# Span-attention steps moved to other stretches by their TensorE tiling, and the fourth group's projections in four column tiles

## The chip, the cores and the metric

The kernel runs on one core of one Trainium2 chip. The metric is the device time of one execution in microseconds (us), as the median of several runs. The engines that matter are TensorE (PE; its weight loads are shown apart as PEld), VectorE (DVE), ScalarE (ACT) and GpSimd (POOL). SyncE (SP) only issues DMAs.

## The reference

The input is `x` (32 batches of 64 rows, 256 wide) and a context of 32 batches of 1601 keys. Three blocks follow each other, each added to `x`, each after a layer norm; all of it in float32.

```python
# 1. cross attention, 16 heads of 16: the 64 rows of a batch look at its 1601 keys
qh, kh, vh = heads(ln(x) @ wq.T + bq), heads(ctx @ wk.T + bk), heads(ctx @ wv.T + bv)
x = x + softmax(mask(qh @ kh.T / 4)) @ vh @ wo.T + bo
# 2. span attention among the 64 rows of a batch
span, value = ln(x) @ W_span.T, heads(ln(x) @ W_val.T)
mean, soft = sigmoid(span[..., 0]) * 64, softplus(span[..., 1])
x = x + softmax(-soft * (pos - mean) ** 2) @ value @ W_out.T
# 3. feed forward: one shared gated unit and two of eight experts per row, chosen by the row's number
x = x + ((silu(h @ sw1 + sb1) * (h @ sw3 + sb3)) @ sw2 + sb2 + experts(h)) / 2
```

Most of the work is in block 1: the projections of 32 x 1601 keys and values, the scores, their exponentials and the product with the values.

## The kernel before, in words

**Halves and groups.** The main loop (L678) runs over 63 of 64 "halves": batch `b` of 32, and in it the heads' half `c` (0 or 1). A half has eight heads in four pairs. The keys are cut into 13 blocks of 124, and the blocks into four groups of 4, 3, 3 and 3 (`GROUPS`). In turn `n` of the loop the scores of half `n + 1` are made while half `n` is turned into probabilities and half `n - 1` is multiplied by its values. Each turn has four parts, g = 0 to 3; the text calls them **stretches** and numbers them `4 * n + g`.

**TensorE's work in a stretch, in the order of the program.** (1) `scores` (L470), tile `psc`: for each key block four matmuls with 32 rows of the array each, one pair of heads in each row tile, into four PSUM banks. (2) In g = 0: four transposes of the running maximum (`pm`, L515), the projection of the next batch's keys of group 0 (`pk`, L443), and four transposes that spread the maximum along rows (`pb`, L530); then `values(n - 1, 1)` (L554, tile `pvs`), the second half of the product with the values. (3) In g = 1 to 3: `project_keys` of group g (`pk`), and in some stretches `project_values` (`pv`, L459); in g = 3 two of these. (4) `run(4 * n + g)`: steps of other work that are due. After g = 3 comes `values(n, 0)` at the head of the next turn.

**Three tilings of TensorE.** The scores use the array as four row tiles (32 x 128). The product with the values, and the product `po2` of the span attention, use it as four column tiles (128 x 32); `pval` (L244) uses two column tiles (128 x 64). Everything else, all projections and transposes included, uses the whole array. A float32 matmul of the program is two matmul instructions in the profile, each with its weight load, so `pk` in one stretch is four instructions, and a column or row tiled product of four tiles is eight.

**VectorE's work.** For each group, the four additions of the mask (L487), which also take the scores out of PSUM, with up to three running maxima (L508) in between; the last three maxima of a half follow g = 3, and the last of them writes `mx`, which the transposes `pm` read. In g = 0 it takes the column maxima (L522). ScalarE takes `pk` and `pv` out of PSUM and computes the exponentials; GpSimd subtracts the maxima (L539, 3.7 us for one pair of heads).

**The agenda.** Work on 128-row tiles of `x` (two batches) is written as generators: `span_steps` (L209; block 2 and the norm of block 3), `query_steps` (L401; the norm and the query projection of block 1) and `finish_steps` (L621; dividing by the sums, and the transposes to `oT`). A step runs in the stretch that the agenda names, and what it yields says after how many stretches the next one runs. So the order of every engine's instructions is fixed by hand (`manual_schedule`). Since a tile has two batches of two halves, everything repeats every four turns. With turns counted as `n mod 4`, the steps of one tile fall as follows (stretch counted from the turn with `n mod 4 = 0`; 16 and above are in the next round, where the next tile's first steps run as well):

| step, tiles | before |
|---|---|
| `po` (L213), VectorE's addition and norm statistics | 2 |
| norm (ACT), then transposes `tr_h`, then `psp` and `pval` with copies to `vbd` | 3, 4, 5 |
| `z` exponential; twenty small VectorE operations (L271 to L287) | 6; 8 |
| subtract, square and weigh, least, exponential, total (POOL, ACT, DVE) | 9 to 13 |
| transposes `psa` (L315); `po2` (L325) | 15; 16 |
| `po3` (L335) with VectorE's addition and statistics | 17 |
| norm (ACT); transposes `tr_f` (L201) with two VectorE copies (L346) | 18; 19 |
| query: statistics, norm, `tr_q`, `pq` (L413), bias | 5, 6, 7, 8, 9 |

**PSUM.** Six banks are shared by all tiles that `mm_bank` (L92) gives out. Two more hold the sums with the values and the running maximum. A tile's first matmul waits until the bank's last reader is done: VectorE's addition for `psc`, ScalarE's copy for `pk` and `pv`.

**The end.** After the last turn a written-out sequence (L728 to L760) runs the remaining steps between units of the shared feed-forward; then the experts follow (L807 to L841).

## Time and profile before

| | |
|---|---|
| median of 3 runs | 1612.97 us (1610.87 to 1616.4) |
| the profiled execution: its own time, its span | 1611.86 us, 1609.8 us |
| mean granted TensorE clock | 0.993 |
| PE, PEld busy | 96%, 72% of the span |
| DVE, POOL, ACT busy | 78%, 69%, 56% |
| turns of the main loop with n mod 4 = 0, 1, 2, 3 (for n = 16 to 19) | 23.37, 21.94, 22.60, 21.92 us |

The last row is the distance between the starts of the first scores of successive turns, read from TensorE's timeline (391.79, 415.15, 437.09, 459.69 and 481.61 us). An engine's busy share is a mean over the whole span; a wait between two engines shows in the list of waits and in the timeline.

### The profile page before, as it was taken

How to read it: one execution, taken by the hardware profiler on the slowest of the kernel's cores; microseconds unless marked ns; L12 is line 12 of the kernel's file. 1: busy time of each engine (PE TensorE's matmuls, PEld its weight loads, DVE VectorE, ACT ScalarE, POOL GpSimd, SP SyncE). 2: the span in 40 equal slices, each digit the busy share in tenths (PEclk: the TensorE clock that was granted, in tenths of full speed). 3: DMA queues.
4: the chain of work that ended last, by engine and by line, in shares of the span. 5: the costliest groups of instructions: out<-in, count | busy, mean ns of one | idle time of the engine just before them, and what ended most of it. 6: DMA issues, size and time to landing. Idle time of an engine off the chain costs nothing.

```text
span 1609.8 us, 55500 instructions
## 1 busy us (share of the span) xinstructions
PE 1548.2 (96%) x24996; PEld 1159.3 (72%) x24996; DVE 1260.5 (78%) x2700; ACT 900.4 (56%) x1229; POOL 1118.8 (69%) x424
## 2 busy tenths in 40 slices
PE   8999999999999999999999999999999999998999
PEld 5777777777777777777777777777777777764588
DVE  4888879888887889888888879888887889886300
ACT  3555656565665656565565656565565656556411
POOL 1777768768696768768687768868687768862620
PEclk9999999999999999999999999999999999999999
DMA  5111111111110111111111111111111111104200
GB/s 170 55 31 43 34 40 34 49 44 43 49 43 28 43 40 33 50 43 43 50 43 37 36 39 34 49 44 43 49 43 32 39 37 34 34 3 130 78 24 30
DMA packets 52044, 73.32 MB, mean 46 GB/s; under 512 B 3812, under 2 KB 51040, under 8 KB 51680
## 3 DMA queue, kind: packets, MB, share of 16 engines
q1 hardware_dynamic: 50992, 69.00, 14.6%
q8 instruction: 196, 3.21, 0.8%
q10 hardware_dynamic: 816, 0.79, 0.1%
q14 instruction: 40, 0.33, 0.1%
HBM read 65.57 MB, written 4.19 MB: 43 GB/s over the span
## 4 chain that ended last, share of the span: by engine, by line
PE 59%; DVE 37%; issue 2%; ACT 1%; DMA 1%; POOL 0%; ACTq 0%; SPq 0%; DVEq 0%; POOLq 0%
DVE mrun L508 13%; DVE prob L487 13%; PE pv L459 13%; PE pk L443 13%; PE pvs L554 9%; PE psc L478 8%; PE py L832 3%; PE u L583 3%; PE pm L515 2%; PE ph L814 2%; PE pb L530 1%; DVE total L305 1%; DVE least L300 1%; DVE mrun L285 1%; PE pval L244 1%
## 5 line engine op out<-in xcount | busy, mean ns | idle before, releaser
L539 POOL TENSOR_TENSOR prob<-prob,mb 124x1664 f32<-124x1664 f32 x252 | 934.1, 3725 | 323.9 <-ACT mb L534 317.1
L487 DVE TENSOR_TENSOR prob<-psc,madd 124x384 f32<-124x384 f32 (+1 forms) x1024 | 582.2, 582 | 176.0 <-PE psc L478 175.9
L508 DVE TENSOR_TENSOR mrun<-prob,mrun 124x512 f32<-124x512 f32 x704 | 483.4, 687 | 7.0 <-ACT mrun L500 4.0
L443 PE MATMUL pk<-ct,wkT_sb 128*128 128x372 f32 (+2 forms) x1024 | 414.6, 529 | 14.8 <-DMA wkT_sb<-in_wkT 5.3
L544 ACT ACTIVATE prob<-prob 124x1664 f32<-124x1664 f32 x256 | 401.5, 1587 | 15.6 <-POOL prob L539 12.6
L459 PE MATMUL pv<-wvT_sb,ct 128*124 128x256 f32 (+1 forms) x1664 | 388.7, 382 | 0.0
L459 PEld LDWEIGHTS pv<-wvT_sb,ct 128*124 128x124 f32 (+1 forms) x1664 | 313.6, 188 | 80.4 <-DVE prob L487 3.4
L478 PE MATMUL psc<-qbd,kT 32*124 32x128 f32 x6656 | 293.9, 286 | 27.0 <-DVE prob L487 24.1
L478 PEld LDWEIGHTS psc<-qbd,kT 32*124 32x124 f32 x6656 | 230.5, 181 | 102.1 <-DVE prob L487 64.3
L447 ACT ACTIVATE kT<-pk,cols 128x372 f32<-128x372 f32 (+2 forms) x256 | 152.0, 594 | 261.8 <-PE pk L443 261.3
L443 PEld LDWEIGHTS pk<-ct,wkT_sb 128*128 128x128 f32 x1024 | 176.8, 192 | 120.6 <-issue 33.3
L465 ACT COPY v<-pv 124x512 f32<-124x512 f32 (+1 forms) x224 | 124.7, 557 | 222.2 <-PE pv L459 222.2
L554 PE MATMUL pvs<-prob,v 124*17 124x64 f32 x13312 | 212.3, 220 | 0.0
L554 PEld LDWEIGHTS pvs<-prob,v 124*17 124x17 f32 x13312 | 189.9, 98 | 26.9 <-issue 25.4
L834 DVE SCALAR_TENSOR_TENSOR ot<-py,prob 128x256 f32<-128x256 f32 x16 | 6.8, 425 | 75.7 <-PE py L832 75.7
L583 PE MATMUL u<-xfT,sw_sb 128*128 128x512 f32 x128 | 57.4, 599 | 0.4 <-DVE xfT L346 0.4
L530 PEld LDWEIGHTS pb<-cst,mc 128*124 128x124 f32 x256 | 29.6, 134 | 35.7 <-DVE mc L522 30.0
L515 PE MATMUL pm<-cst,mx 124*128 124x124 f32 x256 | 40.3, 280 | 8.7 <-DVE mx L508 7.8
L508 DVE TENSOR_TENSOR mx<-prob,mrun 124x512 f32<-124x512 f32 x64 | 43.9, 686 | 2.2
L821 ACT ACTIVATE hT<-ph,cols 128x256 f32<-128x256 f32 x32 | 13.4, 471 | 56.2 <-PE ph L814 56.2
L583 PEld LDWEIGHTS u<-xfT,sw_sb 128*128 128x128 f32 x128 | 23.6, 190 | 27.4 <-issue 24.8
L522 DVE TENSOR_REDUCE mc<-pm 128x4 f32<-128x496 f32 x64 | 42.5, 664 | 0.8 <-PE pm L515 0.8
(126 smaller groups left out, 1133.7 us busy)
## 6 DMA issues: line engine op xcount, KB each, us to landing
ct<-in_ctxT SPq DMA_DIRECT2D x64, 372.0 KB, 3.2
ct<-in_ctxT SPq DMA_DIRECT2D x32, 496.0 KB, 3.5
ct<-in_ctxT SPq DMA_DIRECT2D x32, 361.0 KB, 3.1
w<-in_w SPq DMA_DIRECT2D x16, 256.0 KB, 6.1
x<-in_x SPq DMA_DIRECT2D x16, 128.0 KB, 2.1
x_kept<-x SPq DMA_DIRECT2D x16, 128.0 KB, 1.7
prob<-x_kept SPq DMA_DIRECT2D x8, 256.0 KB, 5.5
out<-ot SPq DMA_DIRECT2D x16, 128.0 KB, 1.9
```

Of the source, the lines that this page charges most:

```text
L443: nc.tensor.matmul(ps[:, :kn], lhsT=wkT[:, i, c * P : (c + 1) * P], rhs=cts[b][g][:, i, :kn], start=(i == 0), stop=(i == 1),)
L447: nc.scalar.activation(kTs[c][:, k0 : k0 + kn], ps[:, :kn], AF.Identity, bias=cols[:, B_K + c : B_K + c + 1])
L459: nc.tensor.matmul(ps[:kn, n * D : (n + 1) * D], lhsT=cts[b][g][:, i, k0 : k0 + kn], rhs=wvT[:, i, :], start=(i == 0), stop=(i == 1),)
L465: nc.scalar.copy(vs[b % 2][:kn, 2 * u : 2 * u + n, :, :DK], ps[:kn, : n * D].rearrange("p (n h d) -> p n h d", n=n, d=DK),)
L478: nc.tensor.matmul(ps[:CHUNK, k * P : (k + 1) * P], lhsT=kTs[c][32 * j : 32 * j + 32, at : at + CHUNK], rhs=qbd[b // 2][32 * j : 32 * j + ...
L487: nc.vector.tensor_tensor(pair_of(n, j)[:, c0 : c0 + nb, :].rearrange("p k (e q) -> p k e q", e=2), ps[:CHUNK, : nb * P].rearrange("p (k e ...
L508: nc.vector.tensor_tensor(dst, block_of(n, k), run, ALU.max)
L515: nc.tensor.transpose(ps[:, j * CHUNK : (j + 1) * CHUNK], m[:CHUNK, j, :], ident[:CHUNK, :CHUNK])
L539: engine.tensor_tensor(sj, sj, m[:CHUNK, j, None, :].to_broadcast([CHUNK, NKC, P]), ALU.subtract)
L544: nc.scalar.activation(pair_of(n, j), pair_of(n, j), AF.Exp)
L554: nc.tensor.matmul(pvs[32 * j : 32 * j + DK + 1, c, :, r, :], lhsT=v[:kn, k, 8 * c + h, :], rhs=pair_of(n, h // 2)[:kn, k, (h % 2) * S : ( ...
L583: nc.tensor.matmul(ps, lhsT=w[:, c, hc * P : (hc + 1) * P], rhs=xfT[:, c, :, slot], start=(c == 0), stop=(c == 1),)
```

## The change

Four things change. The projections of keys and values in stretches with g = 3 are issued as four column tiles of 32 (the new helper `product`). `pval` is issued as four column tiles of 32 in place of two of 64. The steps of stretch `4 * n` run before `values(n - 1, 1)` and no longer after it. The distances between the steps of `span_steps` come from a table, `WAITS` (for the last two tiles `CLOSE`), the exponential of `z` stands before `pval`, and `query_steps` starts one stretch later.

```diff
+    WAITS = (1, 1, 1, 1, 1, 1, 1, 1, 1, 1, 1, 3, 3, 1, 1, 1)
+    CLOSE = (1, 1, 1, 1, 0, 2, 1, 1, 1, 1, 1, 2, 1, 1, 1, 1)
     def span_steps(t: int, oT):
+        waits = iter(CLOSE if t >= NTILE - 2 else WAITS)
...
-        yield 1
+        yield next(waits)
...
+        yield next(waits)
+        nc.scalar.activation(z, z, AF.Exp, scale=-1.0)
+        yield next(waits)
         pval = mm_bank(f"pval_{t}")
         for b in range(2):
             for c in range(2):
-                for e in range(2):
+                for j in range(4):
+                    e, i = divmod(j, 2)
                     nc.tensor.matmul(
-                        pval[e * S : (e + 1) * S, b * P : (b + 1) * P],
-                        lhsT=hT[:, c, b * S : (b + 1) * S], rhs=wvalT[:, c, e * P : (e + 1) * P],
-                        start=(c == 0), stop=(c == 1), tile_position=(0, e * S),
+                        pval[32 * j : 32 * j + 32, b * P : (b + 1) * P],
+                        lhsT=hT[:, c, b * S + 32 * i : b * S + 32 * i + 32],
+                        rhs=wvalT[:, c, e * P : (e + 1) * P],
+                        start=(c == 0), stop=(c == 1), tile_position=(0, 32 * j),
                     )
...
-        yield 1
-        nc.scalar.activation(z, z, AF.Exp, scale=-1.0)
-        yield 2
+        yield next(waits)
...
+    def product(out, lhsT, rhs, start: bool, stop: bool, tiled: bool):
+        n = lhsT.shape[-1]
+        for at in range(0, n, 32) if tiled else (0,):
+            end = min(at + 32, n) if tiled else n
+            nc.tensor.matmul(
+                out[at:end], lhsT=lhsT[:, at:end], rhs=rhs, start=start, stop=stop,
+                **(dict(tile_position=(0, at)) if tiled else {}),
+            )
...
     def run(stretch: int):
         for steps in agenda.pop(stretch, []):
-            wait = next(steps, None)
+            while (wait := next(steps, None)) == 0:
+                pass
             if wait:
                 agenda[stretch + wait].append(steps)
...
-            agenda[4 * n + 1].append(query_steps(b // 2 + 1))
+            agenda[4 * n + 2].append(query_steps(b // 2 + 1))
...
                 m = maxima_along_rows(turned[1])
+                less_maxima(n, 0, m, nc.gpsimd)
+                run(4 * n)
                 if n:
                     values(n - 1, 1)
...
-                project(project_keys, c, g)
+                project(project_keys, c, g, g == 3)
...
                     for u in range(5 if c else 1, 7 if c else 3):
-                        project(project_values, u)
-            less_maxima(n, g, m, nc.gpsimd)
-            run(4 * n + g)
+                        project(project_values, u, True)
+            if g:
+                less_maxima(n, g, m, nc.gpsimd)
+                run(4 * n + g)
```

In the order in which the two built programs hold TensorE's instructions, the steps then fall so: `tr_h` stays in stretch 4 and `psp` in 5, `pval` goes from 5 to 7, `psa` from 15 to 16, `po2` from 16 to 19, `po3` from 17 to 20, `tr_f` from 19 to 22, `tr_q` from 7 to 8 and `pq` from 8 to 9. In stretches with g = 0 they stand between `pb` and the product with the values, in stretches with g = 3 between `pv` and it.

More of the change, by code (lines that the diff above doesn't have):

```diff
@@ L223, in span_steps @@
         nc.scalar.copy(hT, ps)
-        yield 1
+        yield next(waits)
         psp = mm_bank(f"psp_{t}")
@@ L237, in span_steps @@
         )
+        yield next(waits)
+        nc.scalar.activation(z, z, AF.Exp, scale=-1.0)
+        yield next(waits)
         pval = mm_bank(f"pval_{t}")
@@ L253, in span_steps @@
             )
-        yield 1
-        nc.scalar.activation(z, z, AF.Exp, scale=-1.0)
-        yield 2
+        yield next(waits)
         def small(tag: str):
@@ L287, in span_steps @@
         nc.vector.scalar_tensor_tensor(soft, s1, 0.0, acc, ALU.max, ALU.add)
-        yield 1
+        yield next(waits)
         full = [P, H, S]
@@ L294, in span_steps @@
         )
-        yield 1
+        yield next(waits)
         nc.scalar.activation(sc, sc, AF.Square)
         nc.gpsimd.tensor_tensor(sc, sc, soft[:, :, None].to_broadcast(full), ALU.mult)
-        yield 1
+        yield next(waits)
         least, total = small("least"), small("total")
@@ L301, in span_steps @@
         nc.gpsimd.tensor_tensor(sc, sc, least[:, :, None].to_broadcast(full), ALU.subtract)
-        yield 1
+        yield next(waits)
         nc.scalar.activation(sc, sc, AF.Exp, scale=-1.0)
-        yield 1
+        yield next(waits)
         nc.vector.tensor_reduce(total, sc, AX.X, ALU.add)
@@ L307, in span_steps @@
         nc.gpsimd.tensor_tensor(sc, sc, total[:, :, None].to_broadcast(full), ALU.mult)
-        yield 2
+        yield next(waits)
         scf = sc.rearrange("p h k -> p (h k)")
@@ L317, in span_steps @@
             nc.scalar.copy(dst, ps)
-        yield 1
+        yield next(waits)
         po2 = mm_bank(f"po2_{t}")
@@ L331, in span_steps @@
         nc.scalar.copy(o2T.rearrange("p c t -> p (c t)"), po2[:, : 2 * P])
-        yield 1
+        yield next(waits)
         po3 = mm_bank(f"po3_{t}")
@@ L340, in span_steps @@
         nc.sync.dma_start(out=x_kept[t], in_=x)
-        yield 1
+        yield next(waits)
         xn = normalised(x, spread, f"f{t}")
-        yield 1
+        yield next(waits)
         ps = transposed(xn, f"f{t}")
@@ L435, in load_context, with project_keys @@
             load_x(t)
-    def project_keys(b: int, c: int, g: int):
+    def product(out, lhsT, rhs, start: bool, stop: bool, tiled: bool):
[6 more added lines that the diff above has]
+            )
+    def project_keys(b: int, c: int, g: int, tiled: bool = False):
         c0, n = GROUPS[g]
@@ L442, in project_keys @@
         for i in range(2):
-            nc.tensor.matmul(
-                ps[:, :kn], lhsT=wkT[:, i, c * P : (c + 1) * P], rhs=cts[b][g][:, i, :kn],
-                start=(i == 0), stop=(i == 1),
+            product(
+                ps[:, :kn], wkT[:, i, c * P : (c + 1) * P], cts[b][g][:, i, :kn],
+                i == 0, i == 1, tiled,
             )
@@ L449, in project_keys, with project_values @@
         )
-    def project_values(b: int, u: int):
+    def project_values(b: int, u: int, tiled: bool = False):
         blocks = range(2 * u, min(2 * u + 2, NKC))
@@ L458, in project_values @@
             for i in range(2):
-                nc.tensor.matmul(
-                    ps[:kn, n * D : (n + 1) * D],
-                    lhsT=cts[b][g][:, i, k0 : k0 + kn], rhs=wvT[:, i, :],
-                    start=(i == 0), stop=(i == 1),
+                product(
+                    ps[:kn, n * D : (n + 1) * D], cts[b][g][:, i, k0 : k0 + kn], wvT[:, i, :],
+                    i == 0, i == 1, tiled,
                 )
```

## The prediction

> **What bounds the kernel now.** I read the page first, then TensorE's timeline of whole turns, then the list of waits.

> ```profile
> PE 1548.2 (96%) x24996; PEld 1159.3 (72%) x24996; DVE 1260.5 (78%) x2700; ACT 900.4 (56%) x1229; POOL 1118.8 (69%) x424
> ```

> TensorE is nearly always busy, but a busy matmul row is not proof of a bound, so look at the starts in one turn (n = 33, n mod 4 = 1). Columns: start, time, engine, line, operation.

> ```profile
> 780.01 1.65 PE L554 MATMUL pvs<-prob,v 124*17 124x64 f32 x104
> 781.59 0.44 PE L201 MATMUL tr_h<-cst,xn_h 128*128 128x128 f32 x2
> 781.96 0.93 PE L478 MATMUL psc<-qbd,kT 32*124 32x128 f32 x24
> 782.83 1.52 PE L443 MATMUL pk<-ct,wkT_sb 128*128 128x372 f32 x4
> 784.18 1.89 PE L459 MATMUL pv<-wvT_sb,ct 128*124 128x256 f32 x8
> 785.91 0.53 PE L227 MATMUL psp<-wspanT_sb,hT 128*128 128x32 f32 x4
> ...
> 789.61 1.89 PE L459 MATMUL pv<-wvT_sb,ct 128*124 128x256 f32 x8
> 791.43 0.93 PE L478 MATMUL psc<-qbd,kT 32*124 32x128 f32 x24
> 792.29 1.48 PE L443 MATMUL pk<-ct,wkT_sb 128*128 128x361 f32 x4
> 793.61 2.75 PE L459 MATMUL pv<-wvT_sb,ct 128*124 128x256 f32 x12
> 796.20 0.38 PE L201 MATMUL tr_q<-cst,xn_q 128*128 128x128 f32 x2
> 796.51 1.65 PE L554 MATMUL pvs<-prob,v 124*17 124x64 f32 x104
> ```

> No start is late for a semaphore here: the twelve `pv` before `tr_q` take 12 x 0.216 us, and the `pv` at 784.18 gives way to untiled `psp` after 8 x 0.216 = 1.73. What is left over lies where the tiling changes. The same eight `pv` before row-tiled `psc` take 1.82: 0.09 more. `psc` to `pk` is 0.86, of which six groups of four at 0.109 are 0.65: 0.21 more (0.10 entering, 0.11 leaving). `pk` from 782.83 takes 1.35 where four matmuls at 0.3125 take 1.25: 0.10 more for the first weights. `tr_q` to `pvs` is 0.31 for 0.21 of work. So row to whole array costs 0.213 us, whole array to row 0.194, whole array to columns 0.108, columns to row 0.212 and columns to whole array 0.165 (this one, with the change to row behind `tr_h`, in the 1.95 from 780.01 to 781.96).

> In turns with n mod 4 = 0 something else comes in:

> ```profile
> 405.65 0.48 PE L478 MATMUL psc<-qbd,kT 32*124 32x128 f32 x2
> 406.37 0.48 PE L478 MATMUL psc<-qbd,kT 32*124 32x128 f32 x4 [0.24 <-DVE prob L487]
> 407.43 0.91 PE L478 MATMUL psc<-qbd,kT 32*124 32x128 f32 x18 [0.58 <-DVE prob L487]
> 408.49 1.48 PE L443 MATMUL pk<-ct,wkT_sb 128*128 128x361 f32 x4
> ```

> The scores of g = 3 should take 0.67 from first to last start and take 2.42: their banks come free only as VectorE adds the mask to group 2. VectorE is continuously busy there, with `oT`, the addition and statistics of `po3` and those of `po`. In this state the clock can fall. In six of these turns (n = 8, 12, 20, 40, 44, 52) a stretch of 3.41 us at half clock follows and the turn takes 25.05 us, not 23.37. One of them, between other columns (busy us and instructions of each engine, then the clock):

> ```profile
> 317.63:321.04 3.41, 3.41 (x8) 2.30 (x7) 3.34 (x10) 0.56 (x1) 2.79 (x2) 0.50 0.00 0
> ```

> So the loop has two phases. From g = 1 to the scores of g = 3 VectorE sets the pace in turns 0, 2 and 3; from there through `pk`, `pv`, `pvs` and the next g = 0 TensorE does, and VectorE waits:

> ```profile
> DVE prob L487 <- PE psc L478: 175.9, 132, 7.5
> PEld psc L478 <- DVE prob L487: 64.3, 144, 0.8
> ```

> A microsecond off TensorE counts only in the second phase (in turn 1 nearly everywhere).

> [...] the 0.09 to 0.21 us above are this trace's price. [...] here 104 `pvs` take 1.46 us, 0.056 per group of four, the rate of one untiled matmul of 64 columns. [...] the trace shows 3.41 us at 0.50.

> **The change, part by part.**

> *Switches.* The built programs hold 696 changes of tiling before and 590 after. Row to whole falls by 62 (now row to columns), whole to columns by 60 (and by 16 for the 64-wide tiles, 0.144 each), columns to whole by 29, whole to row by 16; columns to row grows by 31, and 15 exits from the 64-wide tiles (0.20) go. Row to columns appears nowhere before. Leaving costs 0.11; entering lies between 0.012 (the 17-column weights of `pvs`) and 0.104 (the 128-column weights of `pk`). I take 0.02, as 32 columns are nearer to 17: 0.129. Sum: 62 x (0.213 - 0.129) + 60 x 0.108 + 16 x 0.144 + 29 x 0.165 + 16 x 0.194 + 15 x 0.20 - 31 x 0.212 = 18 us of TensorE's time. At the dear end (0.213) it is 13.

> *Tiled projections.* 31 turns with 20 groups of four and 31 with 16 take the place of as many single matmuls. No row has four tiles with 256 or 361 columns. `pvs`, `po2` and `psc` all cost what an untiled matmul of the same columns costs, so I take 0 extra. Below 0 is excluded[...]; the upper bound is 0.104 per group (weights not hidden), 116 us in all.

> *Moved steps.* Here each of the four turns gets its own sum, at the bank each tile really has.

> Turn 0 (23.37): `psa` (8 x 0.109) comes ahead of `pvs`, `po2` leaves: g = 1 scores 0.42 later. But VectorE loses the addition and statistics of `po3` (403.48 to 404.70: 1.23), so the end of the g = 3 scores moves by 0.42 - 1.23 = -0.81. Behind it TensorE gains 0.10 (first weights of `pk`) and 0.09 (`pv` to `pvs`), loses `po2` 0.44, gains `tr_f` 0.22: **-0.78**.

> Turn 1 (21.94): `po3` (0.86) comes in before `pvs`; `tr_h` no longer switches twice (0.15), and a wait of 0.14 for `mx` goes: g = 1 scores 0.58 later. VectorE's `po3` work fits its wait there (2.46). `pval` leaves g = 1 (1.0), yet the last bank of the g = 2 scores is now that of VectorE's fourth addition, 0.58 later too; the g = 3 scores end 0.47 later. VectorE gets the query statistics (0.8) and the `xfT` copies (0.5) in g = 2, behind what TensorE needs. After that -0.19 as in turn 0, `pval` 0.87 in for `tr_q` 0.22 and its switch: **+0.86**.

> Turn 2 (22.60): VectorE-bound through. It takes the `xnT` copy (0.34 net) before the twenty small operations; `pq` (0.88 and a switch) goes to g = 1, where TensorE waits anyway. The end moves +0.34, less 0.19: **+0.15**, and `mx` ends 0.13 later in the next turn.

> Turn 3 (21.92): +0.13 carried over, `psa` away (0.87), -0.19: **-0.93**. VectorE's `mx` (21.4 after the turn's first scores) is then needed at 22.0, so it doesn't bind; ScalarE's exponential of the last pair ends some 2 us before `pvs` reads it.

> Sum -0.70 per four turns, 14 times: -9.8. Turns 0 to 3 have little agenda and are TensorE-bound: -1.1; the last two -0.5. Nothing moves ahead of a DMA that is waited for: `po3`'s store of `x` goes with it, and is read at the end. GpSimd's power for the norm waited 25.1 us in all behind `po3`; now it stands behind the first subtraction and need not. At the end `pval` follows the exponential; I cost that at 0 (0.5 either way).

> *Clock.* In turn 0 TensorE's idle time from the first g = 3 scores to `pk` falls from 1.97 us to 1.60. Turn 2 has 1.54 and never fell to half clock. So I expect one of the six windows to stay: -5 x 1.68 = -8.4.

> Total -19.8 on the profiled execution's own 1611.86; the median of the runs is 1.1 above that: 1612.97 - 19.8 = 1593.

> **Rivals.**
> - The clock windows stay (turn 0 is still idle enough). For it: 1.60 is hardly above 1.54[...]. Time 1602.
> - VectorE takes it all: turn 0 is not relieved since `psa` delays it, turn 1 loses as computed. For it: VectorE waits only 176 us over 63 turns, and turn 2 hardly at all. Turns 1 to 3 alone give +0.08 x 14 = +1.1, the edges -1.6, and if two windows go, -3.4: 1609.
> - Slower: the weight loads of the column tiles are not hidden behind 256-column matmuls, or the two passes of one tile hold up its neighbours. With 31 x 36 = 1116 groups the gain is gone at 0.018 us per group, a pitch of 0.234 in place of 0.216; at half of the 0.104 it is 1651. Against it: `po2`, with 32-column weights, keeps 0.056 per group.
> - More: all 18 us of switches count and all windows go: 1584.

> **How the numbers follow.** Runs of this kernel differ by 0.3%, which is what a measurement can tell from no change. Main case 0.50; clock stays 0.20; VectorE 0.11 (on the edge, half of it counted as no change); slower 0.12; more 0.07. Faster 0.81, same 0.07, slower 0.12. 1582 holds the good end; the slower case is left out above, so the upper bound of 1611 takes in the VectorE case.

> **What would show it.** Right: in g = 3, `psc` to `pk` short by about 0.1 with groups of four `pv` 0.216 apart, `pv` to `pvs` without a gap; turn 0 near 22.6 and its g = 3 scores 2.0 long; turn 3 near 21.0; turn 1 longer, near 22.8; at most two windows at half clock in the loop. Wrong: a pitch of the tiled groups well above 0.216, turns of 25, or the g = 3 scores of turn 1 waiting over a microsecond.

## The result: 1607.31 us, where 1593 was forecast

The changed kernel takes 1607.31 us (median of 7 runs, 1602.93 to 1609.6), the kernel before 1611.42 in the runs beside it (median of 7, 1610.58 to 1616.4). The medians are 4.1 us apart; the ratio on record for the two sets of runs is 0.996, with a 95% interval of 0.9947 to 0.9973, which is 6.4 us. Either way the kernel is faster, but by a fifth to a third of the 18 to 20 us that were forecast. The profiled execution of the changed kernel took 1604.45 us, its span is 1602.3 at a mean granted clock of 0.998; before, the span was 1609.8 at 0.993.

The page after, engines first (busy us, share, instructions), then the queue that the profile names `instruction` (packets, MB, share of 16 engines):

```profile
PE 1531.0 (96%) x28600; PEld 1101.3 (69%) x28600; DVE 1261.3 (79%) x2700; ACT 897.5 (56%) x1229; POOL 1121.5 (70%) x424
...
q8 instruction: 224, 3.67, 0.9%
```

TensorE has 3604 matmuls more, each with a weight load, and is busy 17 us less. Before, the queue's line read:

```profile
q8 instruction: 196, 3.21, 0.8%
```

Now the same turn as in the prediction (n = 33) on TensorE's timeline after. Columns: start, time, engine, line, operation.

```profile
771.50 1.03 PE L343 MATMUL po<-woutT_sb,o2T 128*128 128x256 f32 x4
772.37 0.38 PE L201 MATMUL tr_h<-cst,xn_h 128*128 128x128 f32 x2
772.68 1.65 PE L571 MATMUL pvs<-prob,v 124*17 124x64 f32 x104
774.26 0.94 PE L495 MATMUL psc<-qbd,kT 32*124 32x128 f32 x24
...
778.66 1.26 PE L495 MATMUL psc<-qbd,kT 32*124 32x128 f32 x24
...
783.25 1.23 PE L495 MATMUL psc<-qbd,kT 32*124 32x128 f32 x24
784.40 1.42 PE L450 MATMUL pk<-ct,wkT_sb 128*32 128x361 f32 x16
785.64 2.77 PE L450 MATMUL pv<-wvT_sb,ct 128*32 128x256 f32 x48
788.23 1.06 PE L255 MATMUL pval<-wvalT_sb,hT 128*32 128x128 f32 x32
789.11 1.64 PE L571 MATMUL pvs<-prob,v 124*17 124x64 f32 x104
```

In the last stretch four kinds of work follow each other in one tiling: the twelve groups of four `pv` take 788.23 - 785.64 = 2.59 us, 0.216 each, as the untiled ones did. `pk` takes 1.24 to the first `pv`, where it took 1.32 before. So the column tiles cost nothing extra here and the switches are gone. The scores at 778.66 and 783.25 now take 1.2 in place of 0.93: they wait for banks, as computed for turn 1. In turn 0 (n = 16), where the prediction showed 2.42 us from the first to the last start of the scores:

```profile
399.07 0.81 PE L495 MATMUL psc<-qbd,kT 32*124 32x128 f32 x6
400.46 0.91 PE L495 MATMUL psc<-qbd,kT 32*124 32x128 f32 x18 [0.58 <-DVE prob L504]
401.52 1.42 PE L450 MATMUL pk<-ct,wkT_sb 128*32 128x361 f32 x16
```

They now take 2.04. The list of waits (us in total, times, longest) shows the same over the whole span; the second line was 64.3 before:

```profile
DVE prob L504 <- PE psc L495: 175.6, 119, 7.5
...
PEld psc L495 <- DVE prob L504: 48.8, 93, 0.8
```

Turns with the same n mod 4 mostly take the same time to 0.01 us; the text calls this the usual turn of their kind, and what a turn takes beyond it its excess. From one turn's first scores to the next, the usual turn went from 23.37, 21.94, 22.60, 21.92 (n mod 4 = 0 to 3) to 22.59, 22.84, 22.70, 21.11. The changes are -0.78, +0.90, +0.10, -0.81 against -0.78, +0.86, +0.15, -0.93 forecast. All six half-clock windows in the loop are gone. So what was forecast happened; something else took it back. Cut by time, the two profiled executions differ like this: up to the first scores +0.8 (they start between 15.4 and 17.3 us in the kernels here, and a shift of this size comes with edits that don't touch what is ahead of them), the loop -14.2, from the last turn's first scores to the end +5.9 (178.1 to 184.1). Sum -7.5. In the loop, turns 0 to 5 give -2.4, 14 rounds of -0.59 give -8.3 and six windows of 1.68 give -10.1, together -20.8. So 6.6 us lie in turns that were longer than their kind usually is: n = 17 took 23.65, n = 45 took 24.31, where n = 33 took 22.84.

Two things are to be explained, then: 5.9 us at the end and 6.6 us of irregular pauses.

### The profile page after: what moved, and what is told of

The parts are those of the page before. It is cut to its first block, busy times and chain, and to the rows that moved or that the text cites. A ratio compares the mean times of both kernels' runs of the same rounds, so it can differ in the third digit from the quotient of the medians.

```text
span 1602.3 us, 62733 instructions
## 1 busy us (share of the span) xinstructions
PE 1531.0 (96%) x28600; PEld 1101.3 (69%) x28600; DVE 1261.3 (79%) x2700; ACT 897.5 (56%) x1229; POOL 1121.5 (70%) x424
## 3 DMA queue, kind: packets, MB, share of 16 engines
q8 instruction: 224, 3.67, 0.9%
## 4 chain that ended last, share of the span: by engine, by line
PE 60%; DVE 36%; issue 2%; ACT 1%; POOL 1%; DMA 0%; DVEq 0%; POOLq 0%; ACTq 0%
PE pk L450 13%; PE pv L450 13%; DVE mrun L525 13%; DVE prob L504 13%; PE pvs L571 9%; PE psc L495 9%; PE py L853 3%; PE u L600 2%; PE pm L532 2%; PE ph L835 2%; PE pb L547 1%; DVE total L313 1%; DVE least L308 1%; DVE mrun L293 1%; PE pval L255 1%
## 5 line engine op out<-in xcount | busy, mean ns | idle before, releaser
L450 PE MATMUL pk<-ct,wkT_sb 128*32 128x361 f32 (+2 forms) x1768 | 405.5, 499 | 14.9 <-DMA wkT_sb<-in_wkT 5.7
L561 ACT ACTIVATE prob<-prob 124x1664 f32<-124x1664 f32 x256 | 403.1, 1587 | 17.2 <-POOL prob L556 14.3
L450 PE MATMUL pv<-wvT_sb,ct 128*32 128x256 f32 (+3 forms) x4268 | 385.8, 379 | 0.0
L450 PEld LDWEIGHTS pv<-wvT_sb,ct 128*32 128x32 f32 (+3 forms) x4268 | 258.5, 123 | 128.8 <-issue 13.8
L495 PE MATMUL psc<-qbd,kT 32*124 32x128 f32 x6656 | 304.1, 287 | 29.0 <-DVE prob L504 23.4
L495 PEld LDWEIGHTS psc<-qbd,kT 32*124 32x124 f32 x6656 | 240.1, 181 | 96.1 <-DVE prob L504 48.8
L450 PEld LDWEIGHTS pk<-ct,wkT_sb 128*32 128x32 f32 (+1 forms) x1768 | 158.7, 145 | 127.4 <-issue 52.9
L571 PEld LDWEIGHTS pvs<-prob,v 124*17 124x17 f32 x13312 | 195.7, 98 | 20.3 <-issue 10.0
L517 ACT COPY mrun<-prob 124x512 f32<-124x512 f32 x64 | 38.5, 602 | 59.3 <-DVE soft L295 56.1
L532 PE MATMUL pm<-cst,mx 124*128 124x124 f32 x256 | 41.1, 284 | 11.6 <-DVE mx L525 11.6
```

What stands on the lines that cost most here:

```text
L450: nc.tensor.matmul(out[at:end], lhsT=lhsT[:, at:end], rhs=rhs, start=start, stop=stop, **(dict(tile_position=(0, at)) if tiled else {}),)
L495: nc.tensor.matmul(ps[:CHUNK, k * P : (k + 1) * P], lhsT=kTs[c][32 * j : 32 * j + 32, at : at + CHUNK], rhs=qbd[b // 2][32 * j : 32 * j + ...
L532: nc.tensor.transpose(ps[:, j * CHUNK : (j + 1) * CHUNK], m[:CHUNK, j, :], ident[:CHUNK, :CHUNK])
L561: nc.scalar.activation(pair_of(n, j), pair_of(n, j), AF.Exp)
L571: nc.tensor.matmul(pvs[32 * j : 32 * j + DK + 1, c, :, r, :], lhsT=v[:kn, k, 8 * c + h, :], rhs=pair_of(n, h // 2)[:kn, k, (h % 2) * S : ( ...
```

## What the pauses look like

In a long turn TensorE stands still in the middle of a run of matmuls, and in most cases the profile names no semaphore that it waits for. On the timeline of the changed kernel, the bracket holds the idle time before and what released it:

```profile
1036.49 1.02 PE L495 MATMUL psc<-qbd,kT 32*124 32x128 f32 x25
1038.29 0.49 PE L495 MATMUL psc<-qbd,kT 32*124 32x128 f32 x7 [0.78 <-issue]
```

Pauses of this kind come within `psc`, `pk` and `pvs` alike. Numbering all records of TensorE in the trace (matmuls, weight loads, and some 300 waits of its sequencer), each of them begins at a multiple of 256 plus 193. Set beside a usual turn of its kind, matmul by matmul, each of the ten turns that took over 0.3 us too long falls behind within a few instructions of such a place. The instruction queue moved 3.67 MB in 224 packets, 16.4 KB each, for 57,505 such records, so some 256 to a packet, and before 50,267 for 196 packets, again some 256. And in the trace's DMA records a pause ends 2.2 to 3.0 us after the latest of these packets began. So I took the pauses for waits for such a packet; that is my reading of these figures, since no record of the trace names what TensorE waits for there. A block below is a run of 256 of these records, or of as many instructions, from one such place to the next, and such a place is called an edge. Before, four turns had 3076 instructions, 4 more than 12 blocks, so the edges hardly moved against the work, and lay well. After, it is about 3542, 214 more than 13 blocks, and the edges fall somewhere else in each round.

## Experiments

Times are medians, ratios are to the kernel before in runs on the same chip, with the 95% interval. Kernels that ran on different chips are compared by their ratios; against the changed kernel's 0.996 such a difference is uncertain by some 0.2 percentage points.

**1. The end.** The last two tiles' value projection (`pval` and its copies to `vbd`, now the helper `value_rows`) is put back in front of the exponential, in the stretch of `psp`:

```diff
+        closing = t >= NTILE - 2
+
+        def value_rows():
+            pval = mm_bank(f"pval_{t}")
...
+        if closing:
+            value_rows()
         yield next(waits)
...
-        pval = mm_bank(f"pval_{t}")
...
+        if not closing:
+            value_rows()
         yield next(waits)
```

> The changed kernel, but in the last two tiles the value projection of the span attention stands ahead of the exponential again, in the stretch of psp, as before the change. My theory: the late end of the changed kernel (5.9 us more from the last turn's first scores to the end) comes from this order, since ScalarE's copies of pval wait for three units of feed-forward and hold up the gates and the square. Then the stretch from the last turn's first scores to the end falls from 184.1 us to about 179 (178 to 179.8), the transposes psa of the last tile start about 70 us after these scores in place of 75.4, and the time falls by 5 us against the changed kernel, to about 1602. Rival: something else is late next at the end (GpSimd's spans or the gates), so psa stays at 74 to 76 us, and the time stays at 1607.

Measured: 1601.23 us, 0.9927 (0.9916 to 0.9939), so 0.33 percentage points or 5.3 us under the changed kernel's ratio. From the last turn's first scores to the end it is 179.6 us, 4.5 less. ScalarE's timeline in the changed kernel shows what had been late:

```profile
1471.79 0.23 ACT L246 ACTIVATE z<-z 128x32 f32<-128x32 f32 x1
1479.50 0.74 ACT L262 COPY vbd<-pval 64x256 f32<-64x256 f32 x2 [7.49 <-PE pval L255]
1480.26 1.28 ACT L627 ACT_TABLE_LOAD   x1
1481.56 1.27 ACT L627 ACTIVATE prob<-u,cols 128x512 f32<-128x512 f32 x2
1482.72 1.05 ACT L304 ACTIVATE sc<-sc 128x1024 f32<-128x1024 f32 x1
```

and with the old order at the end:

```profile
1469.35 0.73 ACT L258 COPY vbd<-pval 64x256 f32<-64x256 f32 x2
1470.11 1.24 ACT L630 ACTIVATE u<-u,cols 128x512 f32<-128x512 f32 x2
1471.36 1.28 ACT L268 ACT_TABLE_LOAD   x1
1472.66 0.23 ACT L268 ACTIVATE z<-z 128x32 f32<-128x32 f32 x1
...
1477.14 1.06 ACT L312 ACTIVATE sc<-sc 128x1024 f32<-128x1024 f32 x1 [1.32 <-POOL sc L308]
```

In the changed kernel `pval` is issued one stretch later, and at the end units of the feed-forward are begun between the two stretches. `pval` comes behind their matmuls, ScalarE's copies of it wait 7.49 us, and behind these copies wait the gates and the square of `sc`. The square is 5.6 us earlier with the old order, and so is what follows from it. The rival, that something else would be late next, is out. The rest of the 5.9 us is 1.4. About 0.7 of it goes with a second half-clock window of 3.41 us that this execution has near 1445 us: the kernel of experiment 2 has that window too, with the end as before, and takes 178.8 there in place of 178.1. The other 0.7 stays open.

**2. The blocks' edges moved under the kernel before.** The kernel before had next to no such pauses (the excess of its turns 6 to 59 is 0.1 us in all, windows aside), so they can be brought about there:

```diff
+    pad = mm_bank("pad")
+    for _ in range(36):
+        nc.tensor.transpose(pad[:4, :4], ident[:4, :4], ident[:4, :4])
     for g in range(len(GROUPS)):
         scores(0, g, BETWEEN[g])
```

> The kernel before, with 36 transposes of 4 x 4 elements (72 instructions) in front of the first scores, where TensorE waits 1.2 us for ScalarE anyway. Its four turns have 3076 instructions, which is 4 more than 12 blocks of 256, so its edges hardly move from round to round, and they lay at harmless places. My theory: the shift by 72 puts one of them behind the 208 instructions of a product with the values; by the trace of before, a block that takes 2.45 us to come then costs 4 us in all, one that takes 2.6 us costs 7 to 10. So the time is 1615 to 1620, and pauses appear that the kernel before hadn't. Rival: 0 to 1 us above before.

Measured: 1622.56 us, 1.0061 (1.0044 to 1.0077): 9 to 10 us slower for 1 us of work that lies in a wait. Twelve pauses appear, from 215.95 us on, one in each round of four turns until 1223.88 us, 11.4 us in all, every one at the same place modulo 256; the half-clock windows in the loop are six, as before. The list of waits of this kernel has two lines that the kernel before doesn't have, and one of the pauses on the timeline:

```profile
PE psc L478 <- issue: 4.6, 8, 0.9
...
PE po L325 <- issue: 3.8, 4, 1.4
```

```profile
395.79 0.69 PE L478 MATMUL psc<-qbd,kT 32*124 32x128 f32 x11
397.13 0.70 PE L478 MATMUL psc<-qbd,kT 32*124 32x128 f32 x13 [0.65 <-issue]
```

The rival (0 to 1 us) is out. Nothing in the loop was touched; only the number of instructions ahead of it.

**3. The edges held in place under the changed kernel.** In each fourth turn 42 instructions are added, so that four turns are 14 blocks; and once more with all edges shifted by 112 (56 transposes ahead of the first scores, as in 2):

```diff
         ps = mm_bank("pm")
+        for _ in range(21 if n % 4 == 3 else 0):
+            nc.tensor.transpose(ps[:4, 4 * CHUNK : 4 * CHUNK + 4], ident[:4, :4], ident[:4, :4])
```

> The changed kernel with 21 transposes of 4 x 4 elements more in each fourth turn (n mod 4 = 3), in front of the transposes pm, where TensorE waits for VectorE. They make TensorE's instructions of four turns 3584, 14 blocks of 256. My theory: the pauses without a waited-for semaphore in the loop (about 6.6 us in all) are late instruction blocks of 256, and in the changed kernel the block's edge falls at another place of each round, some of them inside dense work; with 3584 it stays at one set of places, which in the trace are 2.5 us or more apart. Then the pauses at index 193 of 256 all but go (under 1 us in all), and the time falls by about 6 us against the changed kernel, to 1601 (1599 to 1604). Rival: the pauses come from something else (context loads, semaphores that the profile lacks), so they stay, and the time is 1607 to 1608 with the transposes' own 0.5.

Measured: 1602.67 us, 0.9935 (0.9923 to 0.9947), 4.0 us by ratio under the changed kernel. The excess of turns 6 to 59 fell from 6.7 to 3.75 us, not to under 1. In the profiled execution, the slowest of the five runs, that gain was lost again: turns 3, 5 and 60 took 2.1 us more, and the end 3.9 us more, with further half-clock windows there. The pauses now come at one and the same `pk` behind the scores of g = 3 in each round, up to 1.1 us in the first rounds, fading later: by the trace's DMA records the packet began there when TensorE had less than 100 instructions left to the edge, and my estimate had assumed that it begins when the block before is entered.

> The same as the pinned kernel, with 56 more transposes of 4 x 4 elements (112 instructions) in front of the first scores, where TensorE waits 1.2 us for ScalarE anyway. They shift the edges of all blocks by 112 instructions against the work. My theory: the edges now fall, in each round, into places where the trace shows 256 instructions within some 1.9 to 2.2 us, so a pause of 0.3 to 0.7 us comes back once or twice in each of 15 rounds: 7 to 12 us more than the pinned kernel, about 1610. Rival: no instruction blocks matter, and it is 0 to 1 us above the pinned kernel.

Measured: 1603.65 us, 0.9941 (0.9926 to 0.9955). This expectation failed: no difference to the unshifted one can be told, and the excess over the usual turns of the unshifted kernel is 3.5 us. Pauses of 0.2 to 0.7 came in eight rounds, in others there was none, though the 256 instructions before the edge had run in 1.8 us. So fixed edges were better than moving ones, but which place is good I could not yet tell from the changed kernel's trace.

**4. Both mended.** The edits of 1 and 3 together:

> The kernel with the values first at the end, and with the 21 small transposes in each fourth turn (3584 instructions in four turns). If the two effects add, it is the pinned kernel less 4.5 to 5 us: 1598 (1596 to 1600), and the stretch from the last turn's first scores to the end is about 180. Rival: the pinned kernel was faster for another reason (its start was 1.5 us earlier in the profile, and its pauses were not fewer), then it is as the kernel with the values first, 1601.

Measured: 1594.83 us, 0.9895 (0.9879 to 0.9911), excess 2.4 us. The two add up within the intervals, and the end is 180.0 us: with them the kernel is near where the prediction had put the change alone (1593).

**5. The moves without the tiles, and the tiles without the moves.** First, the kernel of experiment 1 with `pk` and `pv` of g = 3 untiled (`pval` keeps its four tiles):

```diff
-                project(project_keys, c, g, g == 3)
+                project(project_keys, c, g)
...
-                        project(project_values, u, True)
+                        project(project_values, u)
```

> The kernel with the values first at the end, without the column tiles in the pk and pv of g = 3; all moved steps stay. By the prediction's prices each of 62 turns then pays 0.19 us more (row to whole array and whole array to columns in place of row to columns): +11.8 us; the instruction pauses shrink from some 6 to some 3 us, since 432 fewer instructions in four turns are fetched; no half-clock window comes back. So about 1610 (1607 to 1613), turns of about 22.8, 23.0, 22.7 to 22.9 and 21.3. Rival: what the tiles save in switches their instructions cost again in pauses, and the time is 1600 to 1604, as with tiles.

Measured: 1607.41 us, 0.9974 (0.9964 to 0.9983), 7.6 us by ratio above experiment 1. The usual turns are 22.78, 23.03, 22.87, 21.04: +0.19, +0.19, +0.17 and -0.07. So the price of 0.19 was right to 0.02 in three turns; in turn 3 nothing is gained, which I take for VectorE's last maximum (not tested). The windows stayed away, so these tiles have no part in that. The pauses did not shrink to 3 us as expected: the excess is 6.7, in experiment 1 it is 8.1.

Then the kernel before with `product` and tiled projections in g = 3, and no step moved (the diff is that part of the change alone):

> The kernel before, with only the pk and pv of g = 3 in four column tiles; all steps stay where they were. In turns 0, 1 and 3 a step with whole-array work (tr_f, tr_q, psa) then stands between the tiled pv and pvs, so columns to whole array (0.165) and whole array to columns (0.108) are paid behind the saved 0.19: +0.08 for each of these turns, -0.19 for turn 2 at most, about 0 to +1 us in all; the half-clock windows stay; the pauses for instruction blocks rise from 1 to some 5 us, as 3508 instructions in four turns move the edges through all places. So 1614 to 1619, against 1613 for before. Rival: the tiles pay by themselves, and it is 1605 or less.

Measured: 1620.55 us, 1.0048 (1.0031 to 1.0064). Usual turns 23.45, 22.03, 22.41 and 22.25: +0.08, +0.09, -0.19, +0.33. By the ratio that is 7.7 us more, beyond the expected 1 to 6. Turns 0 to 2 are as the switch prices say; turn 3, forecast at +0.08, with `psa` between `pv` and `pvs`, lost 0.25 more than they say, which I did not follow up. Seven windows are in the loop. Here the tiles pay only when the steps are placed for them, and the steps alone bring the clock.

**6. `po3` back in turn 0.** The kernel of experiment 1 with one number changed, so that `po2` and `po3` run two stretches earlier:

```diff
-    WAITS = (1, 1, 1, 1, 1, 1, 1, 1, 1, 1, 1, 3, 3, 1, 1, 1)
+    WAITS = (1, 1, 1, 1, 1, 1, 1, 1, 1, 1, 1, 3, 1, 1, 1, 1)
```

> The kernel with the values first at the end, with po2 and po3 and what follows two stretches earlier, so that po3 with its addition and statistics falls in g = 2 of turn 0 again, in place of turn 1. My theory of the clock term: VectorE's 1.23 us there make the scores of g = 3 late (first to last start 2.4 in place of 2.0), and half-clock windows of 3.41 us, 1.68 us each, come back in five or more of 15 rounds: +8 to 12 us; the turn sums cancel (turn 0 +0.8, turn 1 -0.9). So 1609 to 1613. Rival: the windows had to do with psa, or with the place of the fetches, and don't come back; then 1601 to 1602.

Measured: 1588.43 us, 0.9855 (0.9838 to 0.9871), 11.6 us by ratio *faster* than experiment 1. This expectation failed: VectorE's load did not by itself bring the windows. The usual turns are 22.98, 21.83, 22.69, 21.10: turn 0 is longer by 0.39 and turn 1 shorter by 1.01, which is -9 us over 15 rounds. The excess is 3.4 us without the turn n = 25, and one window, not five, came into the loop. It came in just that turn, from 593.00 us, and TensorE had paused for 1.66 us at a block's edge until 592.05. The timeline shows turn 0 (n = 16):

```profile
396.32 1.03 PE L351 MATMUL po<-woutT_sb,o2T 128*128 128x256 f32 x4
397.19 1.03 PE L218 MATMUL po<-woP_sb,oT 128*128 128x256 f32 x4
398.14 0.49 PE L503 MATMUL psc<-qbd,kT 32*124 32x128 f32 x6
399.04 0.92 PE L503 MATMUL psc<-qbd,kT 32*124 32x128 f32 x18 [0.41 <-DVE prob L512]
```

VectorE's work is back, but TensorE's `po3` now stands right in front of the scores, where it would else have waited for banks: they take 1.54 from first to last start. VectorE's load is as before the change there; TensorE's idle time is not.

**7. The windows by themselves.** If idle time it is, then useless work in that place must remove them. Both kernels of this experiment also have small transposes ahead of the first scores (76 and 72), so that the added instructions don't move the blocks' edges to bad places. First I put the work behind `po3`:

```diff
         nc.sync.dma_start(out=x_kept[t], in_=x)
+        for c in range(2 if t < NTILE - 1 else 0):
+            nc.tensor.matmul(
+                po3[:, D : 2 * D], lhsT=o2T[:, c, :], rhs=woutT[:, c, :], start=True, stop=True
+            )
...
+    pad = mm_bank("pad")
+    for _ in range(76):
+        nc.tensor.transpose(pad[:4, :4], ident[:4, :4], ident[:4, :4])
```

> The kernel before with work added: behind po3 two more float32 matmuls of 256 columns into the unused half of its bank, read by nobody (0.86 us of TensorE in each fourth turn), so that TensorE is busy in place of idle ahead of the scores of g = 3 in turn 0; and 76 small transposes ahead of the first scores, to keep the instruction blocks' edges at harmless places (0.1 to 2 us of pauses by the trace). My theory: the six half-clock windows in the loop follow the idle time there, 1.97 us from these scores' first start to pk; it falls to 1.1, the turn stays 23.37 since VectorE sets its end, and the windows go: -10 us from the profile with six windows, so 1602 to 1606. Rival: [...] they stay, and the time is 1612 to 1616.

Measured: 1621.6 us, 1.0067 (1.0054 to 1.0079). The time is some 16 us above the expected range. No window is left in the loop, but the added matmuls wait 1.4 us for VectorE's addition to read the bank, and the four turns take 91.06 in place of 89.83 us. The edit was bad for its purpose, so once more in front of `po`:

```diff
         po = mm_bank(f"po_{t}")
+        for c in range(2 if t < NTILE - 1 else 0):
+            nc.tensor.matmul(
+                po[:, D : 2 * D], lhsT=oT[:, c, :, :], rhs=woP[:, c, :], start=True, stop=True
+            )
...
+    pad = mm_bank("pad")
+    for _ in range(72):
+        nc.tensor.transpose(pad[:4, :4], ident[:4, :4], ident[:4, :4])
```

> The test of the half-clock windows once more, with the two added matmuls (0.86 us, read by nobody) in front of the po product, where they wait for nobody: behind po3 they had waited some 1.6 us for VectorE's addition, and made the turn longer. In turn 0 they fill the time between po and the scores of g = 3, which start 0.86 us later while their last start stays where VectorE sets it. 72 small transposes at the start keep the edges of the instruction blocks at harmless places (0.1 to 2 us of pauses by the trace), and cost 0.4 us there. Theory: the six windows go with TensorE's idle time (1.97 us falls to 1.1), turn 0 is 23.37 in every round: -10 us, so 1600 to 1605. Rival: the windows stay, or the turn gets longer by the added work, and it is 1611 or more.

Measured: 1604.29 us, 0.9951 (0.9933 to 0.9969), and all six runs within 1604.16 to 1604.74, while the kernel before ran from 1608.35 to 1618.14. The kernel before gets faster by 0.86 us of work in each fourth turn that nobody reads. The transposes are not what did it: the kernel before had next to no pauses to lose, and with 36 of them alone (experiment 2) six windows stayed. The timeline in turn 0 (n = 16):

```profile
402.11 1.03 PE L213 MATMUL po<-woP_sb,oT 128*128 128x256 f32 x4
402.98 1.03 PE L217 MATMUL po<-woP_sb,oT 128*128 128x256 f32 x4
403.93 0.49 PE L482 MATMUL psc<-qbd,kT 32*124 32x128 f32 x6
404.85 0.92 PE L482 MATMUL psc<-qbd,kT 32*124 32x128 f32 x18 [0.43 <-DVE prob L491]
```

The first line is the added work. The scores now take 1.56 us from first to last start, where they took 2.42. The four turns take 89.84 (89.83 before), with no window in the loop: what the loop gained is the clock alone.

In the trace of the kernel before, the seven half-clock windows last 3.413 us each and start 27, 53, 132, 27, 53 and 69 times 3.413 us after one another. Only six of 15 rounds lost the clock. As an estimate from that trace, let its loop be divided into stretches of 3.413 us, counted from these starts, and let each matmul count with 0.216 us per 256 columns, divided by the number of tiles in its tiling (as four `pvs` of 64 columns take 0.056). Then the six stretches ahead of the six windows in the loop hold 1.08 to 1.23 us of work, and every other one from turn 6 on holds 1.26 or more; with the useless matmuls the least is 1.50. No threshold follows: in experiment 2 stretches with 1.30 and 1.35 kept the clock and stretches with 1.47 and 1.53 lost it. What sets off a window was not shown; the wait of 1.4 us behind `po3` in each fourth turn of the run above did not bring one. In the runs of the kernel before beside this one, 1608.35 us came with a mean granted clock of 0.994 and 1618.14 us with 0.988; there is no trace of those runs.

**8. Experiment 6 with good and with bad edges.** `po3` in turn 0, the values first at the end, and the 21 transposes of experiment 3; with 64 or 112 transposes ahead of the first scores. The places were chosen from the trace of experiment 6.

> The kernel with po3 in turn 0 (and the values first at the end), with the 21 small transposes in each fourth turn and 64 more in front of the first scores (128 instructions, 1.8 us at 14 ns each, of which some 1.2 us lie in a wait). Its edges of 256 instructions should now lie, in every round, at places that the trace of that kernel shows harmless: if a block takes 2.45 us to come, 0.2 us of pauses in all, 1.5 us at 2.8, 7 at 3.2. The kernel without these transposes had some 5 us. So 1583 to 1587, against 1588.4. Rival (the pauses have nothing to do with where the edges lie): 1588 to 1590.

> The same with 112 transposes (224 instructions) in front of the first scores: only the place of the edges differs, and 1.4 us at the start. By the same trace its edges lie at the worst places: 3.7 us of pauses at 2.45 us, 13 at 2.8, 25 at 3.2. So 6 to 14 us above the one with 128: 1592 to 1599. Rival: 1.4 us above it.

Measured: 1582.92 us, 0.9828 (0.9813 to 0.9843), and 1592.06 us, 0.9881 (0.9865 to 0.9896). In one the excess is 0.3 us over turns 6 to 59; in the other the turn with n mod 4 = 0 takes 23.52 (median of 13) in place of 22.98, with a pause in most rounds, such as this one within `pvs`:

```profile
390.79 1.45 PE L581 MATMUL pvs<-prob,v 124*17 124x64 f32 x87
392.60 0.29 PE L581 MATMUL pvs<-prob,v 113*17 113x64 f32 x4 [0.37 <-issue]
```

The two programs differ by 48 transposes of 4 x 4 before the loop begins, 1.1 us later first scores, and 9.1 us. The rival is out. The first of the two is the fastest kernel here: 1.7% under the kernel before, 1.3 percentage points under the change.

## Why the prediction was wrong

**Switches and tiles: right.** "Sum: ... = 18 us of TensorE's time" counted only in part, as the four sums of the turns had it; "-0.19" per turn is +0.19, +0.19, +0.17 when the tiles are taken out, and nothing in turn 3 (5). The pitch of 0.216 was right, so the slower rival, a dearer pitch, did not occur in the form given: no group takes longer.

**Moved steps: right.** -0.70 per four turns was forecast and -0.59 measured. Turn 1's +0.86 came as +0.90; that loss was avoidable, as 6 shows, since turn 0 had room for `po3` on TensorE.

**Clock: right in size, and right in what it looked at.** Six windows went in the profiled execution, five were forecast, -10.1 against -8.4 us. The prediction went by TensorE's idle time in front of `pk`, 1.97 us falling to 1.60, and in 7 work in this place removed the six windows. That one of six would stay was a guess between 1.54 and 1.97, and its closeness is luck. That VectorE's work in that place is by itself enough to bring the windows back, as I assumed for experiment 6, was wrong. The median run of the changed kernel was at a clock of 0.997, the profiled one at 0.998 and 2.9 us faster, so executions of one kernel differ in clock and time; whether by windows or by pauses, these runs don't show.

**"At the end `pval` follows the exponential; I cost that at 0 (0.5 either way)": this step failed.** It is +4.5 us (1). The step is issued one stretch later, and I did not list what is issued in between on TensorE (three units), and what is queued behind the waiting copies on ScalarE.

**"I take 0 extra" for the tiled projections: this step failed by a term that was not there.** The tiles' time is indeed 0 extra (0.216 us per group), and both bounds looked only there. Their number was not free: about 430 instructions more in each four turns, plus 32 of `pval`, moved the edges of the instruction blocks out of a place where they cost 0.1 us over the loop to everywhere, at 6.7 us (2, 3, 8). That is the tiles' doing only in part: with the moves alone (some 3110 instructions in four turns, 38 more than 12 blocks, so the edges travel too) the excess was 6.7, against 8.1 in experiment 1, which differs from it by the tiles alone.

Forecast -19.8 on the span; end +5.9, pauses +6.6, start +0.8, windows -1.7, turns about +0.7: -7.5, as measured. With the end and some two thirds of the pauses mended (4), the time is 1594.8; that this lies so near 1593 is in part chance, since windows, turns and start were off in both directions.

## What to carry to other kernels

When a step moves, list for its new place what is issued between the old and the new one on the same engine, and what stands behind its consumer, at the beginning and end of the program too, where the pattern of the loop doesn't hold. Count instructions as well as their time: where an engine runs hundreds of short ones in a few microseconds (the 208 of one `pvs` took 1.46 us here), look for idle time that no semaphore explains, and at which instruction number it falls. And before work is taken away from the engine that waits, ask whether its idle time costs clock: in 7, filling 0.86 us of it in each fourth turn took the kernel before from 1611.03 to 1604.29 us.
